# Sixteen chunks of 128 source rows fetched row by row from ScalarE's DMA queue instead of by GpSimd's gather

## The chip, the cores and the metric

The kernel runs on one core of a Trainium2 chip. The core has five engines that run beside each other, each through its own instructions in order: TensorE (PE in the profile; its weight loads are PEld), VectorE (DVE), ScalarE (ACT), GpSimd (POOL) and SyncE (SP, which here only issues DMAs). They wait for each other and for DMAs through semaphores. The metric is the device time of one execution in microseconds (us), lower is better.

## The reference

One layer of graph attention over 12,500 nodes and 200,000 edges, sorted by target. Each node's normalised features are turned into 4 heads of 32; each edge has a logit from its source, its target and its own features; a softmax over the edges of a target (and, for the denominator, over all other edges with logit 0) weighs the sources' features, and the sum is added to the node's input.

```python
edge_index = jnp.stack([src, dst])
h = jnp.maximum(_layernorm(x, axis=-1), 0.0)
# inside _L0_gnn_ref(h, edge_index, edge_attr, W_node, W_edge, a):
h = (node_features @ W_node.T).reshape(num_nodes, H, HD)
e = (edge_features @ W_edge.T).reshape(num_edges, H, HD)
att = jnp.sum(jnp.concatenate([h[src], h[tgt], e], axis=-1) * a, axis=-1)
att = jnp.where(att > 0, att, 0.2 * att)
m = jnp.maximum(jax.ops.segment_max(att, tgt, num_segments=num_nodes), 0.0)
ex = jnp.exp(att - m[tgt])
denom = segment_sum(ex, tgt) + (num_edges - deg)[:, None] * jnp.exp(-m)
h_prime = segment_sum((ex / denom[tgt])[:, :, None] * h[src], tgt)
x = x + h_prime.reshape(num_nodes, H * HD)
```

## The kernel before

**Tables.** A first part turns all nodes into rows of `table` in DRAM: 137 numbers of 4 bytes (548 bytes): four heads of 33, and five more, the last four of them the source's share of the logit (`R_SRC`). The edges then need the row of each edge's source.

**Groups, quads, supers.** Edges are cut into 392 groups of 511 (with one carried entry: 512 places, `J` = 4 chunks of `P` = 128). Four groups (`QG`) are a quad; there are 98 quads (`nq`), and `first_fold` is 97. A quad has 16 chunks. Quads are collected into supers, of 4 quads in the middle and of 2, 2, 3 at the start and 3, 3, 2, 2, 1 at the end; the softmax runs once for a super.

**Rows.** `gather` (L171) issues for each chunk one indirect DMA on GpSimd's queue that brings 128 rows of `table` into `ga_all`, a ring of 8 quads (`QUADS`). From quad 8 on it counts landings on one semaphore for each slot of the ring (`arrived`), and `add_sources` waits on that semaphore (L730) before ScalarE copies the sources' shares of the logits out of the rows (`U`, L733). That copy is the first reader of a quad's rows. From quad 16 on the chunks of a quad go out in the order of `order`, with chunk (3, 0) first; chunk (3, 3) is then the last of its quad. The indices lie in SBUF from the start (`srci`).

**Order.** All instructions stand in an order written out by hand: the helpers are Python generators, and `together` takes one step of each in turn. For a quad q, `open_logits(q)` starts the gathers of quad q + 2 (`fetch`, L625); `all_logits(q)` makes the logits of the quad's groups with VectorE (`targets`, L656) and TensorE (L686, L689); its `flush()` calls `add_sources(q - 1)`, which first copies finished logits (`tg`, L699) and then waits for the rows of quad q - 1 and copies `U`. `softmax(s)` is a chain that goes back and forth between the engines: TensorE adds `U` to the logits (L790), ScalarE makes `low` (L795, L800), VectorE takes running maxima, ScalarE makes `fac` (L857) and `stack` (L869), TensorE turns them (L881), ScalarE copies `xs` (L887).

**Sums.** `sums(q)` (L1039) runs some four quads behind the logits: in each of four steps i it weighs the rows of a group (L1067), marks which row belongs to which target (`hot`, L1069), and lets TensorE add them up in PSUM (L1100). Up to quad 74 a window of targets is shared by two or four groups; from quad 75 each group has its own window, and each step closes the window before it (`complete`, L1112): ScalarE copies a carried row (L919), TensorE adds it (L911), ScalarE copies the sum out (`pt`, L979). The rows in the ring are read last here, so a slot is free when the sums of its quad are through.

**Other queues.** SyncE issues the loads and stores of edge features, target places, node windows and results (`issue`, L592). For DRAM rows whose number is known only at run time it loads the number from SBUF into registers (`windows`, L580, a TENSOR_LOAD in the profile) and moves it into the DMA (a MOVE). ScalarE issues a handful of DMAs in all (L262 to L268, L404 to L406, and one-off loads in `checked`, L1450 and L1474, and `parted`, L1148).

**Free memory.** `db_all` (L375) holds target places. From quad 10 on (`OFFSETS`) a quad needs only the first quarter of its half of it.

Of the kernel before, what the change touches and what calls it, by code (L numbers as in the profile page):

```python
# [9 lines left out]
F32 = mybir.dt.float32  # L10
# [4 lines left out]
OP = mybir.AluOpType  # L15
AX = mybir.AxisListType

P = 128
# [28 lines left out]
SQUARE = 32  # L47
TWO = 2
HELD = 3
SETS = max(NODE_T, QG * J)  # L50
PAD = 1 << 20

# [17 lines left out]
def kernel(  # L70
# [39 lines left out]
    nc = tc.nc  # L110
# [53 lines left out]

    spare = consts.tile([P, 6 * SBG * H], F32, name="spare")
    ga_all = consts.tile([P, QUADS, QG, J, ROW], F32, name="ga")
    GA, GATHERED = {}, set()
    arrived = [tc.alloc_semaphore(f"rows{k}") for k in range(QUADS)]
    landings = {}

    def gather(q, rows, width, lo, hi):  # L171

        g0, m = quads[q]
        ga = GA[q] = ga_all[:, q % QUADS]
        chunks = lambda i: -(-min(E - (g0 + i) * NE + 1, GE) // P)
        for i in range(lo, hi):
            if chunks(i) < J:
                nc.vector.memset(ga[:, i, chunks(i):, :], 0.0)
        order = [(i, j) for i in range(lo, hi) for j in range(chunks(i))]
        if q >= 2 * QUADS:  # L180
            order.sort(key=lambda at: at != (hi - 1, 0))
        for i, j in order:
            came = nc.gpsimd.indirect_dma_start(  # L183
                out=ga[:, i, j, 0:width], out_offset=None, in_=rows,
                in_offset=bass.IndirectOffsetOnAxis(ap=srci[:, g0 + i, j:j + 1], axis=0))
# [359 lines left out]
    with tc.tile_pool(name="work", bufs=2) as work, \  # L545
# [87 lines left out]
        def fetch_rows(s):  # L633
            g0, m = groups(s)
            dr = DR[s] = turned.tile([SBG * H, NE + 2], I32, name="dr", bufs=2)
            if finer(s) > 1:
# [4 lines left out]
            nc.sync.dma_start(dr[0:H * m, :],  # L641
                              dst_rows[g0:g0 + m, :].unsqueeze(0).to_broadcast([H, m, NE + 2]))

        def open_logits(q):
            if q == supers[of_quad[q]][0]:
                fetch_rows(of_quad[q])
            if q + 2 < nq:
                fetch(q + 2)
            AT[q] = work.tile([P, QG, GE], BF16, name="at")
# [68 lines left out]
        def add_sources(q):  # L718

            s = of_quad[q]  # L720
            g0, m = quads[q]
            s0, sm = groups(s)
            keep_logits(q)
            if s not in U:
                U[s] = turned.tile([P, J, SBG * H], F32, name="U", bufs=2)
            f = finer(s)
            u = U[s][:, 0:J // f, 0:sm * H * f].rearrange("p c (h w) -> p w c h", h=H)[
                :, (g0 - s0) * f:(g0 - s0 + m) * f]
            if q >= QUADS:
                nc.scalar.wait_ge(arrived[q % len(arrived)],  # L730
                                  sum(landings[a] for a in range(QUADS, q + 1)
                                      if a % len(arrived) == q % len(arrived)))
            taken = nc.scalar.copy(u, GA[q][:, :m].rearrange("p g (f c) r -> p (g f) c r", f=f)[  # L733
                :, :, :, R_SRC:R_SRC + H])
            if q >= QUADS:
                tc.declare_no_dep(taken.ins, group=f"rows{q}",
                                  reason="a semaphore counts the gathers of this quad")
                tc.declare_fence(taken.ins, group=f"rows{q}")
            for kept in (EA, DB, PW, AT):
                del kept[q]  # L740
# [298 lines left out]
        def sums(q):  # L1039
# [36 lines left out]
            for i in range(m):  # L1076
                g = g0 + i
                if first_fold - 4 <= q < first_fold - 4 + FOLDS:
                    shifts(q + 4, i)
                on_gpsimd = early and (q, i) > (first_fold - 2, QG - 2)  # L1080
                if (q, i) not in AHEAD:
                    weighed(nc.gpsimd if on_gpsimd else nc.vector, ga, i,
                            heads(XE[s] if on_gpsimd else ex)[:, :, :, g - s0])
                    if not early:
                        mark(q, i, hot)
                new = i % k == 0
                if not i and not later:
                    entered()
                    settled()
                if new:  # L1090
                    second = k == 2 and i > 0
                    if not second:
                        bank = ps.tile([P, 512], F32, name="acc", bufs=3)
                    acc = bank[0:1 + span, ROW:2 * ROW] if second else bank[0:1 + span, 0:ROW]
                    fc = fac if g == s0 else None
                if later and i == m - 1:
                    entered()
                least_j = 1 if k == 1 else 0
                for j in range(least_j, J)[::-1]:
                    nc.tensor.matmul(acc, hot[:, i, j, 0:1 + span], ga[:, i, j, :],  # L1100
                                     start=new and j == J - 1 and not second,
                                     stop=k > 1 and i % k == k - 1 and j == least_j,
                                     skip_group_check=k > 1)
                if i == (2 if later else 1):
                    passed_on(fac if g0 == s0 else None)
                    if later:
                        settled()
                if not later and i == (2 if k > 1 else 1):
                    entered()
                    if k == 1:  # L1110
                        settled()
                complete(new)  # L1112
                if k == 1:
                    begun.append((q, i, ga, hot, pt, acc, fc))
                if i == 2 and QUADS <= q < first_fold - 5 and of_quad[q + 1] == s:
                    READY[q + 1] = marks(q + 1)
                    beside_rows(q + 1)
                    RESTED.add(q + 1)
                if k > 1 and i == m - 1:
                    state["pending"] = q, bank  # L1120
                if QUADS <= q < first_fold - 5:
                    if i % TWO == 0 and (q, i + 1) not in AHEAD and i + 1 < m:
                        weighed(nc.vector, ga, i + 1, heads(ex)[:, :, :, g + 1 - s0])
# [706 lines left out]
```

## Time and profile before

| | |
|---|---|
| median of 3 runs | 1998.37 us (1998.31 to 1999.74) |
| the profiled execution | 2000.29 us |
| its span, first to last instruction | 1998.4 us |
| mean granted TensorE clock | 0.732 |
| GpSimd busy | 1496.4 us, 75% |
| VectorE busy | 1195.9 us, 60% |
| TensorE busy, matmuls | 1145.4 us, 57% |
| ScalarE busy | 320.7 us, 16% |
| DMA, mean | 115 GB/s |

Busy time does not count DMA issues, register loads and moves of an engine's queue; the profile lists them apart (ACTq, SPq). The profile also names, for each idle stretch of an engine, what ended it. A wait for several semaphores is put down to the one that came last. In the views, "128x137" is partitions x elements, and "ga<-table,srci" reads "written <- read".

### The profile page before, as it was taken

The page shows a single profiled execution, that of the slowest core. Times are in us where ns is not written, and L with a number is a line of the kernel's source. Part 1 is how long each engine was busy: PE and PEld are TensorE (multiplying, and loading weights), DVE is VectorE, ACT ScalarE, POOL GpSimd, SP SyncE. Part 2 cuts the span into 40 slices and gives each one's busy share as a digit, 9 for nine tenths or more (in the row PEclk, how much of TensorE's full clock was granted, in tenths as well). Part 3 has the DMA queues.
Part 4 walks back from the last instruction along what each step waited for, and adds up shares of the span by engine and source line. Part 5 has one row for each costly group of instructions (what it writes and reads, how often), then busy time and mean ns, then how long its engine had stood idle before and what let it go on. Part 6 is the DMA issues. An engine that isn't in the chain of part 4 may idle for free. (4 is left out here: it accounts for less than half of the span.)

```text
span 1998.4 us, 18710 instructions
## 1 busy us (share of the span) xinstructions
PE 1145.4 (57%) x5116; PEld 779.1 (39%) x5116; DVE 1195.9 (60%) x2695; ACT 320.7 (16%) x1077; POOL 1496.4 (75%) x1596
## 2 busy tenths in 40 slices
PE   6566676555464555564646555646464554465565
PEld 5444354334243333343434333434343333234344
DVE  8676787456365554563755646637556465468585
ACT  6564111001001010010010100100101011122122
POOL 7777777777777777777777777777777777777775
PEclk9788788677676776766767767667677677777777
DMA  7754754434344434444444444444443453445441
GB/s 253 208 134 99 174 135 115 101 97 112 95 111 101 119 98 109 101 109 111 115 104 120 98 116 103 110 111 116 103 117 94 106 123 95 123 98 123 101 98 42
DMA packets 167746, 229.56 MB, mean 115 GB/s; under 512 B 60827, under 2 KB 100669, under 8 KB 167638
## 3 DMA queue, kind: packets, MB, share of 16 engines
q0 software_dynamic: 50112, 109.61, 24.9%
q1 hardware_dynamic: 115824, 116.14, 20.3%
q10 hardware_dynamic: 1702, 2.59, 0.4%
q8 instruction: 41, 0.67, 0.1%
q14 instruction: 67, 0.55, 0.1%
HBM read 210.74 MB, written 17.43 MB: 114 GB/s over the span
## 5 line engine op out<-in xcount | busy, mean ns | idle before, releaser
L183 POOL DMA_INDIRECT ga<-table,srci x1494 | 1413.2, 946 | 456.6 <-issue 427.1
L1100 PE MATMUL acc<-ga,hot 128*113 128x137 f32 (+1 forms) x2928 | 544.7, 346 | 95.3 <-DVE hot L1009 55.2
L1100 PEld LDWEIGHTS acc<-ga,hot 128*113 128x113 f32 (+1 forms) x2928 | 484.5, 215 | 193.4 <-issue 80.2
L947 DVE SCALAR_TENSOR_TENSOR pt<-pt,spare,acc 1x133 f32<-1x133 f32 x113 | 38.3, 339 | 517.9 <-ACT den_of L941 516.5
L689 PE MATMUL lg<-at,pw 112*96 112x512 bf16 (+2 forms) x392 | 156.4, 435 | 271.7 <-DVE at L656 257.5
L686 PE MATMUL lg<-ea,by_pair 128*96 128x512 f32 (+1 forms) x392 | 230.8, 674 | 11.4 <-ACT tg L699 11.4
L656 DVE TENSOR_TENSOR at<-const_ps,db 112x1024 bf16<-112x1024 f32 (+1 forms) x176 | 212.7, 1209 | 5.0 <-DMA db<-offset 4.1
L1067 DVE TENSOR_TENSOR ga<-ga,ex_ps 128x1056 f32<-128x1056 f32 x147 | 182.3, 1240 | 0.0
L790 PE MATMUL t_ps<-ident,U 128*64 128x128 f32 (+2 forms) x210 | 46.6, 393 | 196.5 <-ACT U L733 196.5
L733 ACT COPY U<-ga 128x64 f32<-128x64 f32 x98 | 29.0, 298 | 756.4 <-DMA ga<-table,srci 756.1
L1069 DVE TENSOR_TENSOR hot<-const_ps,slot 128x896 f32<-128x896 f32 (+1 forms) x147 | 144.2, 981 | 0.0
L881 PE MATMUL ex_ps<-ident,stack 128*128 128x128 f32 x105 | 28.8, 427 | 188.8 <-DVE stack L871 176.2
L790 PEld LDWEIGHTS t_ps<-ident,U 128*64 128x64 f32 (+2 forms) x210 | 37.1, 200 | 221.7 <-ACT U L733 216.1
L881 PEld LDWEIGHTS ex_ps<-ident,stack 128*128 128x128 f32 x105 | 18.6, 215 | 202.9 <-ACT stack L869 202.9
L689 PEld LDWEIGHTS <-pw 112*96 112x96 bf16 (+2 forms) x392 | 54.4, 139 | 104.4 <-issue 101.9
L966 PEld LDWEIGHTS acc<-pt,spare 1*2 1x2 f32 x226 | 14.0, 86 | 207.9 <-issue 199.6
L183 POOL DMA_INDIRECT ga<-in_x_dram,srci x72 | 68.3, 949 | 23.3 <-issue 18.9
L1026 DVE TENSOR_TENSOR ga<-ga,ex_ps 128x528 f32<-128x528 f32 x92 | 63.5, 693 | 36.5 <-ACT xs L887 36.5
L699 ACT COPY tg<-lg 96x512 f32<-96x512 f32 (+1 forms) x51 | 29.6, 580 | 291.9 <-PE lg L689 275.0
L715 PE MATMUL t_ps<-tg,of_head 96*64 96x512 f32 (+3 forms) x96 | 71.0, 831 | 3.4 <-ACT tg L699 3.4
L715 PEld LDWEIGHTS t_ps<-tg,of_head 96*64 96x64 f32 (+3 forms) x96 | 11.8, 170 | 153.0 <-issue 146.8
L686 PEld LDWEIGHTS lg<-ea,by_pair 128*96 128x96 f32 (+1 forms) x392 | 63.7, 188 | 18.2 <-ACT tg L699 13.8
(205 smaller groups left out, 1314.0 us busy)
## 6 DMA issues: line engine op xcount, KB each, us to landing
ea<-in_edge_t_dram SPq DMA_DIRECT2D x196, 256.0 KB
ga<-table,srci POOLq DMA_INDIRECT x1494
db<-offset SPq DMA_DIRECT2D x53, 256.0 KB
db<-in_dst_dram SPq DMA_DIRECT2D x20, 320.0 KB
db<-offset SPq DMA_DIRECT2D x35, 160.0 KB
table<-row SPq DMA_DIRECT2D x9, 616.5 KB
xt<-in_x_dram SPq DMA_DIRECT2D x9, 576.0 KB
inputs<-in_x_dram SPq DMA_DIRECT2D x92, 56.0 KB
```

Source lines behind the costliest of these rows:

```text
L183: came = nc.gpsimd.indirect_dma_start(out=ga[:, i, j, 0:width], out_offset=None, in_=rows, in_offset=bass.IndirectOffsetOnAxis(ap=srci[:, ...
L656: nc.vector.tensor_tensor(AT[q][:span, i:i + n, :].rearrange("p g e -> p (g e)"), part_ps[:span].to_broadcast([span, n * GE]), DB[q][:span ...
L686: nc.tensor.matmul(lg, by_pair[:, begin:begin + n], ea[:, i // 2, :], start=half == 0 and i == 0, stop=False, skip_group_check=True)
L689: nc.tensor.matmul(lg, PW[q][:span, begin:begin + n], at[:span, i, :], start=False, stop=full and i == quads[q][1] - 1, skip_group_check=True)
L715: nc.tensor.matmul(TP[s][:groups(s)[1] * H], of_head[supers[s][1], p][:n], tg[:n], start=p == 0, stop=False, skip_group_check=True)
L790: nc.tensor.matmul(t_ps[:R, j * P:(j + 1) * P], u[:, j, :R], ident, start=False, stop=j == C - 1, skip_group_check=True)
L881: nc.tensor.transpose(turned_ps[:, j, :], stack[:, j * P:(j + 1) * P], ident)
L947: nc.vector.scalar_tensor_tensor(to, row(w + at), passing[:, w + at:w + at + 1], own, op0=OP.mult, op1=OP.add)
L1026: engine.tensor_tensor(val, val, weight.unsqueeze(3).to_broadcast([P, J, H, HW]), op=OP.mult)
L1067: nc.vector.tensor_tensor(val, val, weight.unsqueeze(3).to_broadcast([P, TWO * J, H, HW]), op=OP.mult)
L1069: nc.vector.tensor_tensor(hot[:, i:i + TWO, :, 1:1 + span].rearrange("p g j c -> p (g j) c"), lane_ps[:, 0:span].unsqueeze(1).to_broadcast ...
L1100: nc.tensor.matmul(acc, hot[:, i, j, 0:1 + span], ga[:, i, j, :], start=new and j == J - 1 and not second, stop=k > 1 and i % k == k - 1 a ...
```

## The change

Sixteen chunks are taken out of the gathers: always the last chunk (group 3, chunk 3) of a quad, in every fifth quad or so. Their rows are fetched one by one, by plain DMAs of 548 bytes on ScalarE's queue, into two row tiles that lie in the free part of `db_all`; when the quad's turn comes, ScalarE waits for the 128 rows and copies them into the place in the ring that the gather would have filled.

The rows are issued inside the sums, 7 at the end of each step i, from quad 12 to first_fold - 6; a chunk takes 19 steps. At every fourth step of a chunk, ScalarE loads the byte offsets of the next 28 rows (16 the last time) into registers. The offsets come from DRAM, one chunk ahead, as a row of 128 indices on one partition (a DMA on ScalarE's queue), and VectorE multiplies them by 548, once for each chunk, two steps after the DMA was issued (at once for the first chunk). Each chunk has one of three semaphores.

```diff
+SINGLES_FROM = 12
...
-        order = [(i, j) for i in range(lo, hi) for j in range(chunks(i))]
+        order = [(i, j) for i in range(lo, hi) for j in range(chunks(i)) if (q, i, j) not in SINGLE]
...
+        class Singles:
+            def __init__(self, engine, kind, some, j, at):
...
+                self.rows = [free[:, k, 0:ROW].bitcast(F32) for k in range(2)]
+                self.places = [free[0:1, k, 2 * P:3 * P] for k in range(2)]
+                self.steps = -(-P // some)
...
+            def target(self, n):
+                return self.first + n * self.steps // QG
+
+            def chunk(self, n):
+                return self.target(n), QG - 1, self.j
...
+            def advance(self):
+                if self.first is None:
+                    self.first = state["opened"] + -(-self.steps // QG) + 1
+                    self.fetch_places(0)
+                    self.scale_places(0)
+                n, at = divmod(self.step, self.steps)
+                self.step += 1
+                q, i, j = self.chunk(n)
+                if q >= nq - 2:
+                    return
+                if not at:
+                    SINGLE[q, i, j] = self, n
+                    self.fetch_places(n + 1)
+                if at == QG // 2:
+                    self.scale_places(n + 1)
+                lo = at * self.some
+                if at % QG == 0:
+                    upto = min(lo + QG * self.some, P)
+                    self.values = nc.values_load_multi_w_load_instructions(
+                        self.places[n % 2][:, lo:upto], engines=[self.kind], min_val=0,
+                        max_val=(NP - 1) * 4 * ROW,
+                        skip_runtime_bounds_check_because="a node's row")[1]
+                for p in range(lo, min(lo + self.some, P)):
+                    came = self.engine.dma_start(
+                        as_bytes(self.rows[n % 2][p:p + 1, :]),
+                        rows_at(table, self.values[p - at // QG * QG * self.some], 4 * ROW, 1))
+                    came.then_inc(self.semaphores[n % 3], 16)
...
+            def put(self, n, to):
+                nc.scalar.wait_ge(self.semaphores[n % 3], 16 * P * (n // 3 + 1))
+                taken = nc.scalar.copy(to, self.rows[n % 2])
...
+        SINGLES = [Singles(*of, at) for at, of in enumerate([(nc.scalar, mybir.EngineType.Activation, 7, 3)])]
+
         def open_logits(q):
+            state["opened"] = q
...
         def add_sources(q):
...
+            for (a, i, j), (of, n) in list(SINGLE.items()):
+                if a == q:
+                    of.put(n, GA[q][:, i, j, :])
+                    del SINGLE[a, i, j]
             if q >= QUADS:
                 nc.scalar.wait_ge(arrived[q % len(arrived)],
...
         def sums(q):
...
                 complete(new)
+                if SINGLES_FROM <= q < first_fold - 5:
+                    for of in SINGLES:
+                        of.advance()
```

More of the change, by code (lines that the diff above doesn't have):

```diff
@@ L166 @@
     ga_all = consts.tile([P, QUADS, QG, J, ROW], F32, name="ga")
-    GA, GATHERED = {}, set()
+    GA, GATHERED, SINGLE = {}, set(), {}
     arrived = [tc.alloc_semaphore(f"rows{k}") for k in range(QUADS)]
@@ L642, in fetch_rows, with fetch_places, scale_places @@
                               dst_rows[g0:g0 + m, :].unsqueeze(0).to_broadcast([H, m, NE + 2]))
+        class Singles:
+            def __init__(self, engine, kind, some, j, at):
+                self.engine, self.kind, self.some, self.j = engine, kind, some, j
+                free = db_all.rearrange("p k g e -> p k (g e)")[:, :, GE * (1 + at):GE * (2 + at)]
+                self.rows = [free[:, k, 0:ROW].bitcast(F32) for k in range(2)]
+                self.places = [free[0:1, k, 2 * P:3 * P] for k in range(2)]
+                self.semaphores = [nc.alloc_semaphore(f"single{at}_{k}") for k in range(3)]
+                self.steps = -(-P // some)
+                self.step, self.first, self.count = 0, None, {}
+            def target(self, n):
+                return self.first + n * self.steps // QG
+            def chunk(self, n):
+                return self.target(n), QG - 1, self.j
+            def fetch_places(self, n):
+                q, i, j = self.chunk(n)
+                if q >= nq - 2:
+                    return
+                g = quads[q][0] + i
+                at = ((g // 2 * J + j) * 2 + g % 2) * P
+                self.engine.dma_start(self.places[n % 2], src[at:at + P].unsqueeze(0))
+            def scale_places(self, n):
+                if self.target(n) < nq - 2:
+                    nc.vector.tensor_scalar(self.places[n % 2], self.places[n % 2], float(4 * ROW),
+                                            None, op0=OP.mult)
+            def advance(self):
[5 more added lines that the diff above has]
+                self.step += 1
+                q, i, j = self.chunk(n)
+                if q >= nq - 2:
+                    return
+                if not at:
+                    assert q not in GATHERED
+                    SINGLE[q, i, j] = self, n
[14 more added lines that the diff above has]
+                    came.then_inc(self.semaphores[n % 3], 16)
+                    tc.no_tile_sem_insts.add(came.ins.name)
+                    tc.add_to_no_dep_group(f"single{self.j}_{n}", came.ins)
+                    self.count[n] = self.count.get(n, 0) + 1
+            def put(self, n, to):
+                assert self.count[n] == P
+                nc.scalar.wait_ge(self.semaphores[n % 3], 16 * P * (n // 3 + 1))
+                taken = nc.scalar.copy(to, self.rows[n % 2])
+                tc.declare_no_dep(taken.ins, group=f"single{self.j}_{n}",
+                                  reason="a semaphore counts the rows of this chunk")
+                tc.declare_fence(taken.ins, group=f"single{self.j}_{n}")
```

## The prediction

> **What bounds the kernel now.** The page is read first, its costliest groups (section 5: line, engine, operation, count, busy us, mean ns, idle us before them and what ended it); then the instructions of the gather's line by themselves (ns minimum/median/maximum, first and last start).
>
> ```profile
> L183 POOL DMA_INDIRECT ga<-table,srci x1494 | 1413.2, 946 | 456.6 <-issue 427.1
> L733 ACT COPY U<-ga 128x64 f32<-128x64 f32 x98 | 29.0, 298 | 756.4 <-DMA ga<-table,srci 756.1
> ```
>
> ```profile
> L183 POOL DMA_INDIRECT ga<-table,srci x1494: 940/945/1376, 93.8 to 1962.1; - x187
> L183 POOL DMA_INDIRECT ga<-in_x_dram,srci x72: 940/945/1162, 3.3 to 92.3; - x72
> ```
>
> GpSimd issues 1566 gathers from 3.3 to 1962.1 us, one every 1958.8/1565 = 1.25 us, and its idle time between them waits for nothing (427 of 457 us are "issue"). Nothing ever holds it up; so whoever uses the rows waits for it: ScalarE's copy L733, the first reader of a quad's rows, stood 756 us waiting for landings. A gather less is worth 1.25 us wherever the rest keeps that pace.
>
> The timeline of ScalarE (start us, us, instruction, in brackets the idle time before it and who ended it) says where it does. There is one L733 for each quad; counted back from the last (quad 97), these are quads 78, 92, 93, 96 and 97.
>
> ```profile
> 1585.64 0.30 ACT L733 COPY U<-ga 128x64 f32<-128x64 f32 x1 [11.63 <-DMA ga<-table,srci]
> 1866.18 0.30 ACT L733 COPY U<-ga 128x64 f32<-128x64 f32 x1 [10.42 <-DMA ga<-table,srci]
> 1888.11 0.29 ACT L733 COPY U<-ga 128x64 f32<-128x64 f32 x1
> 1948.85 0.30 ACT L733 COPY U<-ga 128x64 f32<-128x64 f32 x1
> 1966.10 0.30 ACT L733 COPY U<-ga 128x64 f32<-128x64 f32 x1 [0.99 <-DMA ga<-table,srci]
> ```
>
> Up to quad 92 the landing sets the pace. From 1866.18 on the work itself does: quads 93 to 96 (the first and last of four are shown) find their rows landed, and quad 97 waits only 0.99 us. So the end follows the start of quad 92 by a fixed 132.2 us of span, and the question is when quad 92 starts.
>
> **The change part by part.** *Removed:* 16 gathers of 1.25 us, 20.0 us of GpSimd. By the step count in the code, chunk n goes to quad 22 + 19n//4 (22, 26, 31 ... 93). Fifteen of the quads lie at or before 92, twelve at or before 78: landings come 15 x 1.25 = 18.7 us earlier at quad 92 and 15.0 us at quad 78.
>
> *Added, on ScalarE's queue:* per row one register load, one register move, one DMA issue; 2048 rows in 304 steps of the sums loop (quads 12 to 87), 6.74 a step on average. ScalarE does none of this 2048 times before, so the prices come from SyncE, which loads row addresses with the same call (one, two and four registers at a time in the three stretches below), and from the two one-row DMAs of ScalarE.
>
> ```profile
> L582 SPq TENSOR_LOAD <-base_row x25: 264/273/291, 304.4 to 769.0; - x25
> L582 SPq TENSOR_LOAD <-base_row x27: 467/475/498, 910.8 to 1432.9; - x27
> L582 SPq TENSOR_LOAD <-base_row x19: 863/872/967, 1617.6 to 1936.5; - x19
> L596 SPq MOVE inputs<-in_x_dram x203: 29/29/38, 132.3 to 1953.7; - x102
> L1450 ACTq DMA_DIRECT2D rows<-in_dst_ends_dram x1: 245/245/245, 426.8 to 426.8; - x1
> L1148 ACTq DMA_DIRECT2D rows<-in_fine_ends_dram x1: 250/250/250, 1804.4 to 1804.4; - x1
> 1703.75 0.35 SPq L596 DMA_DIRECT2D inputs<-in_x_dram  x1
> 1704.20 0.37 SPq L596 DMA_DIRECT2D out_dram<-res  x1
> ```
>
> One, two and four registers take 273, 475 and 872 ns: 0.20 us for each further register, so 28 cost about 5.7 us. A one-row DMA takes 0.25 us; between two issues of SyncE with a move lie 1704.20 - 1703.75 - 0.35 = 0.10 us. A row is therefore 0.20 + 0.25 + 0.10 = **0.555 us**, an estimate from these rows; its bounds are 0.50 (the DMA's 0.245, the move and no more gap than 0.03) and 0.67 (a DMA at SyncE's 0.37). I take the middle price because the two ScalarE DMAs are the nearest rows. The Trainium skill ("DMA: Bandwidth & Descriptors", Latency and other measured facts) gives a register load a floor of some 0.6 us that unrolling spreads out. If 28 registers came for one such floor, a row would be an estimated 0.37 us and this sum would turn into a gain. The three rows above speak against it: the third and fourth register cost as much as the second.
>
> *Does it run beside waits?* What counts is whether ScalarE issues DMAs while an earlier instruction of its own waits. In two places of the trace a DMA or a load with nothing of its own to wait for stands behind a waiting instruction:
>
> ```profile
> 1804.09 0.27 ACT L979 COPY pt<-acc 81x137 f32<-81x137 f32 x1 [0.55 <-PE acc L911]
> 1804.39 0.22 ACT L985 ACTIVATE den<-pt 81x16 f32<-81x16 f32 x1
> 1804.39 0.25 ACTq L1148 DMA_DIRECT2D rows<-in_fine_ends_dram  x1
> ```
>
> ```profile
> L1541 ACTq TENSOR_LOAD <-flag x1: 486/486/486, 1979.8 to 1979.8; - x1
> ```
>
> The DMA starts with L985, which needed the result of L979; it did not go ahead while L979 waited. So a burst that follows a wait in program order starts after it, and hides only what the next wait would have been.
>
> *First stage, quads 12 to 74 in the sums* (the waits of ScalarE by releaser from 326 to 1586 us: us, times, longest):
>
> ```profile
> ACT U L733 <- DMA ga<-table,srci: 673.2, 63, 19.4
> ACT tg L699 <- PE lg L689: 228.4, 30, 9.4
> ACT fac L857 <- DVE fac L856: 84.4, 15, 5.7
> ACT low L800 <- DVE t_ps L798: 55.9, 15, 4.0
> ACT stack L869 <- DVE stack L868: 45.3, 15, 3.0
> ACT low L795 <- PE t_ps L790: 30.9, 15, 2.1
> ACT xs L887 <- PE ex_ps L881: 21.1, 16, 1.3
> ```
>
> Here lie 249 of the 304 steps: 1677 rows x 0.555 = 931 us. What they can fill: the landing waits 673, less the 15 that go; tg 228, which has two bursts ahead of it; both low, 87, and about 40 of fac, each with one burst of 7 rows (2.5 us) ahead. stack and xs have none. That is 1013 us, so ScalarE keeps the landing's pace with 80 us to spare. This cover ends at a row price of 1013/1677 = 0.60 us. Behind a late copy stand den_of, which VectorE waits for, and the rest of a quad; being late by less than the ring of 8 quads allows costs nothing until quad 78.
>
> *Second stage, from quad 78's copy to quad 92's,* 280.5 us, the sums of quads 74 to 87 with one window per group, so that ScalarE copies twice per group around a matmul:
>
> ```profile
> ACT pt L979 <- PE acc L911: 99.4, 56, 5.1
> ACT U L733 <- DMA ga<-table,srci: 81.9, 9, 13.3
> ACT fac L857 <- DVE fac L856: 19.0, 4, 5.6
> ACT stack L869 <- DVE stack L868: 12.1, 4, 3.0
> ACT xs L887 <- PE ex_ps L881: 5.3, 4, 1.3
> ACT ga L925 <- DVE pt L947: 5.0, 1, 5.0
> ACT low L800 <- DVE t_ps L798: 4.6, 2, 4.0
> ACT low L795 <- PE t_ps L790: 2.1, 1, 2.1
> ```
>
> ```profile
> 1669.92 0.27 ACT L979 COPY pt<-acc 81x137 f32<-81x137 f32 x1 [3.98 <-PE acc L911]
> 1687.46 0.27 ACT L979 COPY pt<-acc 81x137 f32<-81x137 f32 x1 [2.89 <-PE acc L911]
> ```
>
> 55 steps, 370 rows x 0.555 = 205.6 us. Without landing waits the stage takes 280.5 - 81.9 = 198.6 us. Of the 99.4 us of pt, 0.55 (the matmul between its two copies, as at 1804.09) stays in each of 56: 30.8. In four softmax quads the 3.98 and the 2.89 stay too, as no burst lies between the copy of U or of xs and them: about 23. Hidden are 99.4 - 54 = 45, of fac about 13 (one burst each, four times), half of ga, both low: **68 us**; bounds 0 and 99 (everything but the 0.55s, stack and xs). The stage then takes 198.6 + 205.6 - 68 = 336 us. Quad 92 starts at 1585.6 - 15.0 + 336 = 1907 instead of 1866.2: **41 us late**, although its rows landed 18.7 us early.
>
> *Small things:* 16 copies of 128x137 on ScalarE (0.27 us each, by L979), 16 VectorE multiplies of one row and 16 fetches of indices: under 0.3 us a quad; taken as nothing, 3 us in the second stage if ScalarE has no room. VectorE's multiply waits for its indices' landing, which was issued two steps ahead, except the first, which holds VectorE and what follows it some 2 us, once, while rows are still awaited. Each copy waits for rows issued about a quad earlier. SyncE's and GpSimd's queues lose no place.
>
> *Sum:* -15 + (336 - 280.5) = +41 on the profiled execution's 1998.4 us of span (1.9 us lie around it; the median of the runs, 1998.37, equals its span). **2039 us.** Under the row's own bounds (0.50 to 0.60) and hidden parts of 50 to 90 this case goes from 2010 to 2080.
>
> **The rivals.** *Faster: ScalarE issues ahead of its waits.* The Trainium skill ("Perfetto Trace Analysis", DVE / Act Engine Instruction) says that an engine instruction is pushed into a wait queue and the sequencer is then free for the next one. As a mechanism here: bursts would run beside pt, fac, stack, xs and low as well, 147 us in the second stage, and 205.6 would fit in 81.9 + 147. Then GpSimd stays the bound: quad 92 starts 18.7 us early, quad 97's 0.99 us of waiting goes too, 1998.4 - 19.7 = **1979 us**. It decides once the hidden part passes 109 us. For it speaks that only starts are seen, and few of them; against it stand 1804.39 and 1979.8. Chance 0.14.
>
> *Faster by price.* The row costs less than (81.9 + 68 + 15)/370 = 0.445 us, from which point the end is not later than before; at 0.38 or less the gain is nearly whole, 1979 to 1985. It needs registers far under 0.20 us; the three L582 rows say no, though none loads 28. Chance 0.12; a price near 0.445, within 0.2%: 0.04.
>
> *Much slower: the first stage overflows too.* Above 0.60 us a row the 80 us of room are gone. At 0.65 the first stage adds 1090 - 1013 = 77 and the second 35 more: 2039 + 112 = **2150 us**. SyncE and ScalarE issuing at once would be the cause; SyncE's 0.35 and 0.37 against ScalarE's 0.25 point that way. Chance 0.12.
>
> **How the numbers follow.** The forecast has 0.58, so slower 0.70, faster 0.26, the same 0.04; 0.2% (4 us) is about what can be told from no change. The likeliest case alone spans 2010 to 2080; the faster cases at 1979 hold too much to be left out, so the range is 1978 to 2085, which leaves the overflow above.
>
> **What would show it.** Right: GpSimd still 1.25 us a gather with 1550 of them; ScalarE's loads of 28 near 5.7 us and its row DMAs some 0.35 us apart; landing waits of L733 shrinking from 673 to about 80 in the first stage and gone from quad 79 to quad 90; quad 92's copy near 1907. Wrong: loads far shorter, DMAs that start while an earlier ScalarE instruction still waits, or L733 waiting for landings up to quad 92; then the time is near 1979. L733 late from the first supers on, with GpSimd waiting for the ring, would be the overflow.

## The result, and the profile after

| | before | after |
|---|---|---|
| median | 1998.34 us | **2008.9 us** (2007.22 to 2011.27, 4 runs) |
| profiled execution, span | 1998.4 us | 2007.3 us |
| quad 78's copy of `U` (end of the first stage) | 1585.64 | 1569.68 |
| quad 92's copy of `U` (end of the second stage) | 1866.18 | 1876.89 |
| rows of the table fetched singly | 0 | 2048 |

The change makes the kernel slower by 10.6 us: ratio 1.0053, interval 1.0041 to 1.0064 (95%). The forecast was 41 us.

GpSimd did what it was to do. The costliest groups of the changed kernel (the gather is now L184, the copy of `U` L813; busy us, mean ns, then idle us before them) show 16 gathers less, the same duration, and landing waits of ScalarE down from 756 to 443 us:

```profile
L184 POOL DMA_INDIRECT ga<-table,srci x1478 | 1397.6, 946 | 450.7 <-issue 428.4
L813 ACT COPY U<-ga 128x64 f32<-128x64 f32 x98 | 29.1, 298 | 521.3 <-DMA ga<-table,srci 442.9
```

The timeline of ScalarE shows where it was given back. These are the copies of quads 78, 91, 92, 93 and 97, counted back from the last:

```profile
1569.68 0.30 ACT L813 COPY U<-ga 128x64 f32<-128x64 f32 x1 [11.30 <-DMA ga<-table,srci]
1866.04 0.30 ACT L813 COPY U<-ga 128x64 f32<-128x64 f32 x1
1876.89 0.30 ACT L813 COPY U<-ga 128x64 f32<-128x64 f32 x1
1899.28 0.30 ACT L813 COPY U<-ga 128x64 f32<-128x64 f32 x1
1975.79 0.30 ACT L813 COPY U<-ga 128x64 f32<-128x64 f32 x1
```

Up to quad 78 a landing sets the pace, 16.0 us earlier than before (forecast: 15.0). From quad 79 to quad 92 no copy of `U` waits for rows any more: the second stage took 1876.89 - 1569.68 = 307.2 us instead of 280.5, and quad 92 is 10.7 us late although its rows were there. After it the end follows as before, by 130.4 us of span (132.2).

The instructions of the two new queue lines (ns minimum/median/maximum, first and last start), and ScalarE's timeline over two steps of the second stage:

```profile
L695 ACTq TENSOR_LOAD <-db x80: 1190/1944/2180, 336.4 to 1854.5; - x80
L700 ACTq DMA_DIRECT2D db<-table x2048: 227/235/690, 338.5 to 1863.5; - x187
```

```profile
1640.33 0.27 ACT L1059 COPY pt<-acc 81x137 f32<-81x137 f32 x1 [1.68 <-PE acc L1180]
1640.40 2.19 ACTq L700 DMA_DIRECT2D db<-table  x7
1642.63 0.22 ACT L1078 CAST hot<-is_last 128x16 f32<-128x16 bf16 x1 [2.03 <-issue]
1642.74 0.32 ACT L1117 COPY ga<-xs 128x80 f32<-128x80 f32 x1
1642.96 0.26 ACT L999 COPY ga<-acc 1x133 f32<-1x133 f32 x1
1643.77 0.27 ACT L1059 COPY pt<-acc 81x137 f32<-81x137 f32 x1 [0.55 <-PE acc L991]
```

Three things are to be seen. A load of 28 addresses takes 1.94 us, 0.07 a register, where the forecast had 0.20. Seven rows with their moves take 2.19 us, 0.313 a row. And the burst starts 0.07 us after `pt` has started, not while `pt` waits (1.68 us) for TensorE; none of the 54 waits of `pt` in this stage has a burst inside it. Behind the burst ScalarE stands 2.03 us with nothing but "issue" as the reason. After the burst the chain carried row (L999), TensorE (L991), `pt` still has its own 0.55 us: the burst hid nothing of it. Elsewhere the wait behind a burst even grows: the 4.48 us of the third row below were 2.17 before the change (1628.13). Behind the burst of 1615.33, `tg` stands 2.03 us, TensorE stands 2.97 us for `tg` and then has logits and sums to do before the matmul that `pt` needs:

```profile
1617.57 0.58 ACT L775 COPY tg<-lg 96x512 f32<-96x512 f32 x1 [2.03 <-issue]
1618.20 2.02 PE L762 MATMUL lg<-ea,by_pair 128*96 128x512 f32 x2 [2.97 <-ACT tg L775]
1622.94 0.27 ACT L1059 COPY pt<-acc 81x137 f32<-81x137 f32 x1 [4.48 <-PE acc L991]
```

The waits of ScalarE from quad 78's copy to quad 92's (us, times, longest), of which the forecast kept 54 us of `pt`:

```profile
ACT pt L1059 <- PE acc L991: 78.0, 54, 5.6
ACT hot L1078 <- issue: 27.6, 10, 4.4
ACT ga L999 <- issue: 20.3, 7, 4.3
ACT fac L937 <- DVE fac L936: 19.7, 4, 5.6
```

The stage holds 369 rows and 14 loads. By the typical burst and the median load they take 369 x 0.313 + 14 x 1.92 = 142.4 us, **0.386 a row**. Its work without landing waits was 198.6; the 307.2 leave 198.6 + 142.4 - 307.2 = 33.8, or **34 us hidden**. The landing waits that the bursts could use up were 81.9 us, so the stage grew by 142.4 - 33.8 - 81.9 = 26.7. Added up one by one, the loads (25 us) and the bursts (122 us; many right behind a load take 2.42 us instead of 2.19) make 147 us, 0.40 a row and 39 hidden; so the two figures are good to about 5 us.

### The profile page after: what moved, and what is told of

The parts are those of the page before. It is cut to its first block, busy times and chain, and to the rows that moved or that the text cites. A ratio compares the mean times of both kernels' runs of the same rounds, so it can differ in the third digit from the quotient of the medians.

```text
span 2007.3 us, 22961 instructions
## 1 busy us (share of the span) xinstructions
PE 1158.1 (58%) x5116; PEld 785.9 (39%) x5116; DVE 1198.1 (60%) x2711; ACT 334.5 (17%) x1093; POOL 1481.1 (74%) x1580
## 5 line engine op out<-in xcount | busy, mean ns | idle before, releaser
L184 POOL DMA_INDIRECT ga<-table,srci x1478 | 1397.6, 946 | 450.7 <-issue 428.4
L762 PE MATMUL lg<-ea,by_pair 128*96 128x512 f32 (+1 forms) x392 | 244.6, 711 | 73.1 <-ACT tg L775 73.1
L813 ACT COPY U<-ga 128x64 f32<-128x64 f32 x98 | 29.1, 298 | 521.3 <-DMA ga<-table,srci 442.9
L991 PE MATMUL acc<-ga,hot 128*81 128x137 f32 x176 | 49.2, 371 | 71.5 <-ACT ga L999 66.0
L184 POOL DMA_INDIRECT ga<-in_x_dram,srci x72 | 68.5, 951 | 23.4 <-issue 18.6
L791 PE MATMUL t_ps<-tg,of_head 96*64 96x512 f32 (+3 forms) x96 | 65.9, 776 | 23.7 <-ACT tg L775 23.7
```

The source lines that it names most:

```text
L184: came = nc.gpsimd.indirect_dma_start(out=ga[:, i, j, 0:width], out_offset=None, in_=rows, in_offset=bass.IndirectOffsetOnAxis(ap=srci[:, ...
L762: nc.tensor.matmul(lg, by_pair[:, begin:begin + n], ea[:, i // 2, :], start=half == 0 and i == 0, stop=False, skip_group_check=True)
L791: nc.tensor.matmul(TP[s][:groups(s)[1] * H], of_head[supers[s][1], p][:n], tg[:n], start=p == 0, stop=False, skip_group_check=True)
L991: nc.tensor.matmul(acc, hot[:, i, 0, 0:acc.shape[0]], ga[:, i, 0, :], start=False, stop=stop)
```

## The experiments

**Theory A**: a gather less is worth 1.25 us to the end, and only the second stage takes it back, because bursts of 0.39 us a row on ScalarE's own queue exceed what waits it has there. **Rivals**: the loss goes with the rows or the small DMAs wherever they lie (B), or with a lower granted TensorE clock in that stage (C). **Theory D** is on the size: why 28 registers cost no more than about nine by SyncE's rows.

### The gathers alone

The 16 chunks are marked as fetched otherwise, and nothing fetches them.

```diff
-    GA, GATHERED, SINGLE = {}, set(), {}
+    GA, GATHERED = {}, set()
+    SINGLE = {(22 + 19 * n // 4, QG - 1, J - 1) for n in range(16)}
...
-                if SINGLES_FROM <= q < first_fold - 5:
-                    for of in SINGLES:
-                        of.advance()
```

> The same 16 chunks are not gathered and nothing fetches them: no loads, no row DMAs, no copies, so 2048 of the rows in the sums are old ones. It prices the removed part alone. Theory A: 15 gathers fewer up to quad 92 and 16 in all at 1.25 us, less what the last quads' own work takes back: 1998.4 - 19.7 = 1979 (1977 to 1982), quad 92's copy at 1866.2 - 18.7 = 1847.5. If the gathers were not what the end waits for, or the second stage is slowed by something that comes with earlier landings (the clock), it would be 1985 to 1998.

Measured: **1979.69 us** against 1997.54, ratio 0.9909 (0.9892 to 0.9925). Quad 92's copy stands at 1846.62, forecast from the gathers 1847.5:

```profile
1846.62 0.30 ACT L809 COPY U<-ga 128x64 f32<-128x64 f32 x1 [10.43 <-DMA ga<-table,srci]
```

The removed part is worth what the prediction says, and the whole of it reaches the end.

### Singles in the first stage alone, and in the second alone

```diff
+SINGLES_TO = 75
...
                 n, at = divmod(self.step, self.steps)
+                if not at and state["opened"] >= SINGLES_TO:
+                    return
```

> The changed kernel, but no new chunk of singles is begun once quad 75's logits are open: 13 chunks instead of 16, all of them read by ScalarE before the sums of quad 74, so none in the second stage. Theory A (the loss is ScalarE's bursts in the second stage, where it has too few waits to put them in): rows land 13 x 1.25 = 16 us earlier from quad 79 on, the second stage keeps the length of before (280 us), and the time is 1998 - 16 = 1982 (1980 to 1986). Rival B (the loss comes with the 2048 small DMAs or the lost gathers themselves, wherever they lie): about 13/16 of the 10.6 us stay, 2004 to 2008. Rival C (the second stage is longer for a lower granted TensorE clock, 0.67 against 0.74): the stage stays above 295 us and the time is 1993 or more.

Measured: **1982.74 us** against 1997.54, ratio 0.9923 (0.9906 to 0.9939). Quads 78 and 92 in ScalarE's timeline:

```profile
1570.12 0.30 ACT L816 COPY U<-ga 128x64 f32<-128x64 f32 x1 [11.46 <-DMA ga<-table,srci]
1849.29 0.30 ACT L816 COPY U<-ga 128x64 f32<-128x64 f32 x1 [9.38 <-DMA ga<-table,srci]
```

The stage is back at 279.2 us and a landing sets its end. For the reverse, only singles from the sums of quad 74 on:

```diff
-SINGLES_FROM = 12
+SINGLES_FROM = 74
```

> The same kernel as in the run e3_late, against a before of about 1998: singles in the second stage alone, three chunks. Theory A: that stage takes 307 us from 1585.6 on, quad 92's copy at 1893, the end at 2025 (2020 to 2030). Rival B (the loss goes with the number of rows): 2000.

Measured: **2024.99 us** against 1997.79, ratio 1.0132 (1.0115 to 1.0149). Three chunks instead of sixteen cost 27 us instead of 10.6. Quad 78 starts as before the change, and quad 92 lies 309.4 us later, one microsecond from the 1893 that was expected:

```profile
1584.58 0.30 ACT L813 COPY U<-ga 128x64 f32<-128x64 f32 x1 [8.68 <-DMA ga<-table,srci]
1894.02 0.30 ACT L813 COPY U<-ga 128x64 f32<-128x64 f32 x1
```

Theory A stands and B falls: thirteen chunks gain, the three in the second stage lose.

### Fewer rows a step

```diff
-        SINGLES = [Singles(*of, at) for at, of in enumerate([(nc.scalar, mybir.EngineType.Activation, 7, 3)])]
+        SINGLES = [Singles(*of, at) for at, of in enumerate([(nc.scalar, mybir.EngineType.Activation, 4, 3)])]
```

> The same kernel as in the run e2_four, against a before of about 1998: 4 rows a step, 9 chunks, loads of 16. Theory A: 55 steps of 1.55 us in the second stage less some 30 hidden fit into its 82 us of landing waits: 1986 to 1988. Rival B (the loss goes with the number of rows): about 2004.

Measured: **1987.84 us** against 1997.79, ratio 0.9953 (0.9936 to 0.9969). Singles run into the second stage here too, and it still waits for landings (ScalarE's waits from 1576 to 1854):

```profile
ACT pt L1059 <- PE acc L991: 86.1, 55, 5.2
ACT U L813 <- DMA ga<-table,srci: 42.8, 8, 11.5
```

So it is not singles in that stage as such: what matters is whether the bursts, less what other waits hide of them, are smaller than its landing waits. The expectation counted 55 steps of bursts there, 85 us; the ninth and last chunk ended at 1768, so the trace has 156 rows and nine loads, 156 x 0.313 + 9 x 1.19 = 60 us.

### The row's price: loads and moves taken out

Each row comes from a fixed place; the DMAs stay.

```diff
-                if at % QG == 0:
...
-                        rows_at(table, self.values[p - at // QG * QG * self.some], 4 * ROW, 1))
+                        as_bytes(table[p:p + 1, :]))
```

> The changed kernel without register loads and moves: each single row is fetched from a fixed row of the table (row p for partition p) with the same DMA, so the rows are other ones. 80 loads of 1.2 to 2.0 us and 2048 moves of 0.03 go, the 2048 DMAs stay. Theory A (a row costs ScalarE about 0.39: 0.31 for DMA, move and gap, 0.07 for the load): a row then costs 0.27 to 0.29, the second stage's 369 rows give back 37 to 44 us, more than the 26.7 us by which that stage grew, so landings bind again at quad 92 and the time is 1979 to 1987. Rival B (contention of the small DMAs with the gathers' traffic, not ScalarE's own time): 2005 to 2010. If the loads cost more than their rows show, the gain would be the whole 19.7: 1979.

Measured: **1985.39 us** against 1997.54, ratio 0.9933 (0.9915 to 0.9951). Seven rows take 2.04 to 2.10 us here, so a row costs about 0.29, 0.10 less, and the change gains: the second stage takes 1852.83 - 1570.83 = 282.0 us. That speaks against contention of the 2048 DMAs, which are all there. The stage's waits still have 78.0 us of `pt`, as in the changed kernel, although the granted clock was 0.72 here and 0.66 there (1570 to 1850 us); so their total doesn't go with the clock. What the clock of rival C adds all the same is worked out further down:

```profile
ACT pt L1053 <- PE acc L985: 78.0, 55, 5.2
ACT U L807 <- DMA ga<-table,srci: 25.6, 3, 11.6
```

### What a register load costs

One load of 7 in each step, instead of one of 28 in four.

```diff
-                if at % QG == 0:
-                    upto = min(lo + QG * self.some, P)
+                if True:
+                    upto = min(lo + self.some, P)
...
-                        rows_at(table, self.values[p - at // QG * QG * self.some], 4 * ROW, 1))
+                        rows_at(table, self.values[p - lo], 4 * ROW, 1))
```

> The changed kernel with a register load of 7 at every step instead of one of 28 at every fourth. The trace of the changed kernel has ScalarE's loads of 16 registers at 1.19 us and of 28 at 1.94: a line of 0.19 + 0.0625 a register. By it a load of 7 takes 0.63, four take 2.5 against 1.94, and the second stage grows by 55/4 x 0.56 = 8 us: 2009 + 8 = 2017 (2012 to 2020). By SyncE's rows (273, 475, 872 ns for one, two, four: 0.2 a register, so that a long load alone is cheap) a load of 7 takes 1.47, four take 5.9: the second stage grows by 55/4 x 3.9 = 54 us: about 2060. If the price of a load is a fixed one, whatever its length: 7.8 for four, above 2070.

Measured: **2073.33 us** against 1997.54, ratio 1.0376 (1.0359 to 1.0393). The straight line through 16 and 28 registers missed by 56 us. The time is the one that was expected of a fixed price, but the loads have two prices. These are the loads by themselves (ns; all, then the two of the steps that begin at words 0 and 7 of a chunk; a word is 4 bytes, one address):

```profile
L695 ACTq TENSOR_LOAD <-db x304: 661/1728/2073, 336.1 to 1922.0; - x152
...
L695 ACTq TENSOR_LOAD <-db x1: 1245/1245/1245, 905.1 to 905.1; - x1
...
L695 ACTq TENSOR_LOAD <-db x1: 1800/1800/1800, 909.0 to 909.0; - x1
```

Those at words 0, 28, 56 take about 1.2 us, those at 7, 14, 21 about 1.8, with the same seven registers; 14 is even and slow, 28 is no multiple of eight and fast. That suggested theory D: from a multiple of four words a load takes four registers in a piece, from elsewhere one. 28 registers are then 7 pieces (1.94 us), 16 are 4 (1.19 at the least in the changed kernel), 7 are 1 + 3 = 4 pieces (1.2) or 7 (1.8). It also covers the SyncE rows of the prediction: 36 + 78 = 114 windows stand before the first load of four, so all of those began two words past a multiple. The test moves the addresses by one word, and SyncE's row bases by two, onto a multiple:

```diff
-    base_row = consts.tile([1, W], I32, name="base_row")
+    base_row = consts.tile([1, W + 2], I32, name="base_row")[:, 2:W + 2]
...
-                self.places = [free[0:1, k, 2 * P:3 * P] for k in range(2)]
+                self.places = [free[0:1, k, 2 * P + 1:3 * P + 1] for k in range(2)]
```

> The changed kernel with the row addresses of the singles stored one word further on, so that each load of 28 starts one word past a multiple of four words; and SyncE's row bases two words further on. Theory D, from the loads of 7 (1.13 to 1.25 us where they begin at a multiple of four words, 1.72 to 1.92 elsewhere) and from 16 and 28 registers in 1.2 and 1.94: a load goes in pieces of about 0.24 us; a piece takes four registers where the load begins at a multiple of four words, and one register otherwise. Then 28 registers off the multiple cost 28 x 0.2 to 0.24 + 0.2 = 5.8 to 7 us instead of 1.94, a row about 0.53 to 0.56 instead of 0.39, the second stage's 14 loads add 55 to 70 us, and the time is 2064 to 2079; and SyncE's loads of four row bases, which so far began two words past a multiple (114 words stand before them), fall from 0.87 to 0.27 to 0.35 us. Rival E (a load of ScalarE has a price of its own, about 1.7 us, whatever it loads, SyncE's another): 2007 to 2012, SyncE's still 0.87. Rival F (only the words up to the next multiple go singly): 10 pieces, 2.6 us, about 2018.

This kernel, and those with 4 and 12 rows and with the second stage alone, ran first beside a kernel before that took 2512 us. All four were slower than it there, the one with 4 rows too (2792, 2622, 2927 and 2560 us). Why isn't known; the same chip gave 1998 us for the kernel before a quarter of an hour later. The four ran again, under names that end in 2, beside a kernel before of 1998 us, and what is said here of gains holds for that.

> The same kernel as in the run e9_shift, where a load of 28 one word off took 6.15 us (median) but the kernel before took 2512 us; here against a before of about 1998. Theory D (pieces of four registers only from a multiple of four words): loads of 28 at 6.0 to 6.4 us, 4.2 to 4.4 more than in the changed kernel; the second stage has 14 of them, nothing left to hide them in: 2009 + 60 = 2069 (2062 to 2078); SyncE's aligned loads of four row bases at 0.27 to 0.35 us instead of 0.87. Rival E (a price of ScalarE's own): 2007 to 2012.

Measured: **2062.79 us** against 1997.79, ratio 1.0325 (1.0308 to 1.0342). ScalarE's loads of 28, and then SyncE's loads of four from 1640 us on; `base_side`, which was left where it was, is the control:

```profile
L695 ACTq TENSOR_LOAD <-db x80: 3602/6246/6417, 335.0 to 1903.1; - x80
...
L583 SPq TENSOR_LOAD <-base_row x19: 276/303/506, 1650.4 to 2015.2; - x19
L583 SPq TENSOR_LOAD <-base_side x13: 867/879/1343, 1653.1 to 1972.5; - x13
```

One word of shift makes the same load 3.2 times as long, 1.94 to 6.25 us, and costs 54 us of the kernel's time (2062.79 against 2008.9); two words of shift, onto a multiple, take SyncE's load of four from 0.87 to 0.30. Rival E falls (a price of ScalarE's own), and F (2.6 us) too. Loads of 16, 20 and 24 that start on a multiple, in the runs with 4, 10 and 12 rows a step, lie between, 0.22 us for each four more registers (medians; the shortest in the last two views, 0.72 us, are the loads of 8 that end a chunk):

```profile
L695 ACTq TENSOR_LOAD <-db x72: 1183/1289/1407, 335.1 to 1758.9; - x72
```

```profile
L698 ACTq TENSOR_LOAD <-db x126: 715/1486/1605, 335.4 to 1486.9; - x126
```

```profile
L698 ACTq TENSOR_LOAD <-db x132: 718/1726/1974, 335.7 to 1652.3; - x132
```

With the addresses shifted a row costs (369 x 0.313 + 14 x 6.25)/369 = 0.55 us, the price of the forecast.

### How much the first stage takes

12 rows a step, a load of 24 in every second step, and the stop of above:

```diff
-        SINGLES = [Singles(*of, at) for at, of in enumerate([(nc.scalar, mybir.EngineType.Activation, 7, 3)])]
+        SINGLES = [Singles(*of, at) for at, of in enumerate([(nc.scalar, mybir.EngineType.Activation, 12, 3)])]
...
-                if at % QG == 0:
-                    upto = min(lo + QG * self.some, P)
+                if at % 2 == 0:
+                    upto = min(lo + 2 * self.some, P)
...
-                        rows_at(table, self.values[p - at // QG * QG * self.some], 4 * ROW, 1))
+                        rows_at(table, self.values[p - at // 2 * 2 * self.some], 4 * ROW, 1))
```

> The same kernel as in the run e7_twelve, against a before of about 1998: 12 rows a step, 22 chunks, none in the second stage. Theory A: 27.5 us of GpSimd go, ScalarE's 2816 rows at 0.39 just fill the first stage, what comes late is caught up in the second: 1970 (1967 to 1976). If bursts of 12 hide less than those of 7 and the first stage overflows by more than the 82 us that the second can catch up: 1985 or more, up to the 2025 that a step cost of 4.7 us on 249 steps gives with nothing but landing waits to hide it in.

Measured: **2060.89 us** against 1997.79, ratio 1.0316 (1.0298 to 1.0333). Missed: quad 78's copy comes at 1672.27, 114 us behind the 1558 of the pace, and the second stage doesn't catch that up, since GpSimd had to stop between gathers. Its waits (us, times, longest), here and in the changed kernel:

```profile
POOL ga L185 <- issue: 525.9, 1480, 8.6
POOL ga L185 <- ACT ga L1120: 9.5, 2, 6.3
POOL ga L185 <- ACT t_ps L843: 7.4, 1, 7.4
```

```profile
POOL ga L184 <- issue: 447.0, 1466, 0.3
```

Between gathers the changed kernel has no pause above 0.3 us; here pauses of up to 8.6 us add up to some 90 us, as much as the time lies above the 1970 that was expected. They can't be made up, because GpSimd runs at 1.25 us a gather without a pause even before. That it stopped for a slot of the ring is read from the code; the profile names no releaser for most of these pauses. This is the prediction's third rival, reached by more rows and not by a higher price. With the same edit at 10 and at 8 rows:

> 10 rows a step (13 steps a chunk, loads of 20 at every second step), no new chunk once quad 75's logits are open: 19 chunks, none in the second stage. A row is 0.34 + 1.4/20 = 0.41 us, so 249 steps are 1021 us against the 1013 us of room that the prediction counted in the first stage (12 rows: 1225, and it overflowed; 7 rows: 715, and it did not). By that room it is just full, what is late is caught up in the second stage, and 19 x 1.25 = 23.7 us of GpSimd go: 1974 to 1977. If the room is smaller (the part of the bursts hidden in fac, low and tg was too large in the second stage, 40 of 68), up to 30% of 1013, the first stage is up to 300 us over and the time is 1990 or more.

Measured: **1976.33 us** against 1998.12, ratio 0.9888 (0.9871 to 0.9904), with 18 chunks, one less than counted: 18 x 1.25 = 22.5. Of the landing waits of the first stage 83 us are left, and quad 92 still waits for its rows:

```profile
ACT U L816 <- DMA ga<-table,srci: 83.1, 18, 17.4
```

```profile
1844.77 0.30 ACT L816 COPY U<-ga 128x64 f32<-128x64 f32 x1 [9.61 <-DMA ga<-table,srci]
```

> 8 rows a step (16 steps a chunk, loads of 16 at every second step), stopped at the same place: 15 chunks. 249 steps of 8 x 0.34 + 0.6 = 3.3 us are 822 us, inside even a room of 85% of 1013: 15 x 1.25 = 18.7 us earlier, 1979 to 1981. Above 1983.5 (the run with 7 rows, stopped at the same place) the room would be under 800 us.

Measured: **1980.58 us** against 1998.12, ratio 0.9909 (0.9893 to 0.9926), 15 chunks. At 10 rows the first stage is nearly full: 2304 rows x 0.41 = 945 us and 83 left make 1028, against the 1013 of the prediction. The kernel with 10 rows is the fastest of all, 22 us below before and 32.6 below the changed one.

### The same singles on SyncE's queue

```diff
-        SINGLES = [Singles(*of, at) for at, of in enumerate([(nc.scalar, mybir.EngineType.Activation, 7, 3)])]
+        SINGLES = [Singles(*of, at) for at, of in enumerate([(nc.sync, mybir.EngineType.SP, 7, 3)])]
```

> The changed kernel with loads, moves and row DMAs of the singles on SyncE's queue instead of ScalarE's; 16 chunks in the same places, the copies into the ring stay on ScalarE. Theory A (only ScalarE's own queue time made the second stage longer): quad 92's copy comes 18.7 us earlier than before, 1979 (1977 to 1983), provided that SyncE keeps up: a step is 7 x (0.33 + 0.03 + 0.1) + 1.94/4 = 3.7 us, four of them 15 us in a quad of 20 us. Rival G (SyncE's queue is in order too: a row issued behind a result's DMA that waits for the softmax comes late, or pushes the edge features and offsets back): 1990 or more.

Measured: **1997.89 us** against 1998.12, ratio 0.9996 (0.9986 to 1.0005). Rival G, and in the profiled execution at one place. Quad 88's copy is at 1768.75, one microsecond from the run without those gathers (1767.81); quad 90's, 1834.31, is 24.7 us later than in that run (1809.58). In between VectorE's timeline has two waits that the kernel before does not have there:

```profile
1804.65 0.68 DVE L1422 TENSOR_TENSOR res<-pt,const_ps 81x512 f32<-81x512 f32 x1 [12.78 <-DMA out_dram<-res]
...
1831.70 1.22 DVE L732 TENSOR_TENSOR at<-const_ps,db 80x1024 bf16<-80x1024 f32 x1 [6.52 <-DMA db<-offset]
```

VectorE's first wait ends 1.9 us behind the last of these three stores of results on SyncE's queue:

```profile
1792.29 0.34 SPq L597 DMA_DIRECT2D out_dram<-res  x1
...
1795.19 2.17 SPq L700 DMA_DIRECT2D db<-table  x7
...
1797.95 0.34 SPq L597 DMA_DIRECT2D out_dram<-res  x1
...
1799.98 2.21 SPq L700 DMA_DIRECT2D db<-table  x7
...
1802.77 0.34 SPq L597 DMA_DIRECT2D out_dram<-res  x1
```

Seven rows lie between one store and the next, and ahead of the first the queue stands 5.0 us, which the profile puts down to the landing of a one-off load of ScalarE; no other kernel here has that wait, and its cause stays open. ScalarE's loss is gone, and SyncE's order takes back the whole gain.

## Why the prediction was right in direction and wrong in size

- **GpSimd as the bound, 1.25 us a gather, the end fixed behind quad 92: right.** Shown by the run without the gathers (1979.69; the rival had 1979), and by quad 78, 16.0 us early for 15.0.
- **The first stage keeps the pace: right.** The forecast left about 80 us of landing waits; at the real price 443 stayed. Its room of 1013 us was a little small: bursts and waits that were left make 945 + 83 = 1028 at 10 rows and 647 + 443 = 1090 in the changed kernel; at 12 rows it overflowed. In the run with the shifted addresses, at the price of the forecast, 173 us of landing waits stayed instead of 80, and quad 78 still waited 6.27 us for its rows at 1569.85.
- **The second stage becomes ScalarE's: right**, with the place (quads 79 to 92). Shown by the two halves of the change run alone. That its loss outweighs the gain came out for another reason than the forecast's, as said below.
- **"0.20 us for each further register, so 28 cost about 5.7 us": this step failed.** A load of 28 took 1.94. The row cost 0.386 instead of 0.555, so 369 rows took 142 us and not 205.6: 63 us less. The three rows it was drawn from have the prices right, but all of those loads of four start off a multiple of four words, so they couldn't show the cheap form. Shifted by a word, the loads took 6.25. The Trainium skill ("DMA: Bandwidth & Descriptors", Latency and other measured facts) would have given an estimated 0.37 a row, close to the 0.386 measured. The nearness is luck, since 28 registers took 1.94 us and not 0.6, and a DMA with its move 0.313 and not 0.35. Its reason, a floor of some 0.6 us spread by unrolling, isn't what the traces show either: single registers took 0.27 on SyncE, and seven took 1.2 or 1.8 us by where they start.
- **"Hidden are ... 68 us": this step failed too, the other way.** 34 to 39 were. 24 us of what is missing show in one row: `pt` kept 78 us where 54 had been left. A burst stands ahead of the copy of the carried row (and of `tg`, as at 1617.57), and that copy, TensorE and `pt` come after it in a chain, which begins when the burst is over. The rest isn't traced to rows. With the shifted addresses the same sum gives 198.6 + 203 - (1928.60 - 1569.85) = 43 hidden. That run had the price forecast and came to 2062.8, not 2039: 24 us for the hidden part.
- **The sign was luck: two errors against each other.** With the price right and 68 hidden the stage would have been 198.6 + 142.4 - 68 = 273 us (278 with the 147), shorter than the landings' own 280.5, and the sum would have said 1979. The rival "faster by price" had the price, and its 1979 to 1985 failed on the hidden part. The break-even price of 0.445 was therefore too high: with 34 hidden it is (81.9 + 34 + 15)/369 = 0.355, between the 0.386 of the change (slower) and the 0.29 of the run without loads (faster). The lower end of the likeliest case was also added up too high: 0.50 a row with 90 hidden gives a stage of 198.6 + 185 - 90 = 293.6 and a time of about 1996, not 2010.
- **No run-ahead of waits: right.** Bursts start 0.07 us behind the start of the instruction ahead of them, as at 1640.40. By the rule from the Trainium skill ("Perfetto Trace Analysis", DVE / Act Engine Instruction) as the rival read it, the 1.68 us ahead of `pt` would have held the burst; the trace doesn't agree.
- **The lower clock (rival C): in part, and in part open.** The second stage was granted 0.66 in the changed kernel, 0.65 with shifted addresses, 0.72 to 0.74 in the runs that gain. This adds to its length: `pt` waits 0.55 us for its matmul where the clock is 1.00 (1643.77) and 0.84 where it is 0.50 (1635.94). Of the 56 `pt` of the stage 21 waited 0.83 or 0.84, against 5 before the change, which is 16 x 0.29 = 4.6 of the 26.7 us. TensorE's whole busy time there grew from 154.3 to 170.6 us, so more than about 16 is unlikely. What lowers the clock wasn't tried.

## What to carry to other kernels

Work moved off a bound engine is paid by stage: here thirteen chunks were free and three cost more than all sixteen gained, so ask of each stage whether the new host still waits for something there, and stop where it doesn't. A wait hides a burst only if the burst stands directly ahead of it in the queue and the waiting instruction's input doesn't come from behind the burst; a chain of copy, matmul, copy kept 78 of its 99 us here. And before a price per item is drawn from small cases, ask what else differs between them than the count, here the address at which they begin.

## What the runs showed of the hardware

- A register load is priced by where it starts (words of 4 bytes in SBUF). From a multiple of four words: 4 registers 0.30 us (SyncE), 16 registers 1.29, 28 registers 1.94 (ScalarE). Off it: 4 registers 0.87 (SyncE), 7 registers 1.8, 28 registers 6.25 (ScalarE).
- A DMA of one row of 548 bytes takes 0.235 us to issue on ScalarE, with its move 0.313 from one to the next within a burst.
- The same short wait for a matmul took 0.55 us where the granted clock was 1.00 and 0.84 where it was 0.50.
